# Two of a norm's four small steps move from GpSimd to VectorE

## The chip, the cores and the metric

The kernel runs on one core of one Trainium2 chip. The metric is the device time of one execution in microseconds. Engines are named as in the profile: PE is TensorE (PEld its weight loads), DVE is VectorE, ACT is ScalarE, POOL is GpSimd and SP is SyncE, which issues most DMAs.

## What is computed

The input x has 4 images of 128 channels and 64 x 64 places, so 4 x 4096 tokens of 128 channels. Two layers follow each other:

- Layer 0: a group norm, then `_L0_conv_ref`: a LayerNorm over channels, a depthwise 3x3 convolution with LayerNorm, GELU and a 1x1 product, a residual and a LayerNorm, then a state-space scan (16 states, 64 inner channels, four chunks of 32 channels) over the 4096 tokens, a LayerNorm, a projection, and a residual.
- Layer 1: LayerNorm, attention with 4 heads of 32 over the 4096 tokens of an image, a residual, LayerNorm, a mixture of 8 experts of which the best two count, and a residual.

What matters here is the LayerNorm without weights, which all of these use:

```python
def _layernorm(x, axis=-1, eps=1e-5):
    m = jnp.mean(x, axis=axis, keepdims=True)
    v = jnp.var(x, axis=axis, keepdims=True)
    return (x - m) / jnp.sqrt(v + eps)
```

## The kernel before

**Tiles.** The tokens of an image are cut into 8 blocks of 512. A block is held as 128 channels x 512 tokens, or, for norms, as 4 tiles of 128 tokens x 128 channels; TensorE transposes between the two. There are 32 blocks (4 images of 8).

**The norm.** `normalised(lane, src)` (line 502) handles one block. DVE makes statistics of the four tiles (`bn_stats` into st, then `bn_aggr` into mv, which holds a mean and a variance for each of the 4 tiles, so 128x4x2 numbers). POOL then makes the factor rs = (variance + EPS)^-0.5 and shift = -mean * rs, each 128x4 numbers, in four instructions: the addition of EPS to the variances (line 512, writes rs), the power with the constant tile mhalf (line 513, in place in rs), the product of mean and rs (line 515, writes shift) and the product of that with -1 (line 516, in place). The function then yields twice and ACT applies the norm to the four tiles with `scalar.activation(..., bias=shift, scale=rs)` (line 521) into xt, which TensorE transposes back. rs, shift, mv and st come from the pool `small` with 4 buffers of each name, and the names carry the lane's letter, X or Y.

Six places call it: `first_norm` (585), `conv` twice (638, 655), `closed` twice (804, 818) and `finished` (1032). Each is called for each of the 32 blocks, which makes 192 norms, 100 of them in lane Y and 92 in lane X.

**The scan's slot.** The work of the scan comes in 1024 units (block, half p, state n). One unit is one slot of the main loop (line 1223): ACT makes the decay da = exp(delta * A) (`decayed`, 742), DVE the product h = rows * du, the running scan over it and the product hc (`scan`, 747), TensorE sums hc over the 16 states in PSUM (y). From slot 128 on (`ALONE`, 1220) POOL first adds the hc of two states, and TensorE sums the pairs. ACT copies the last column of h into `state` for the next block.

**Attention** runs alongside: in each slot a group of two key tiles, with four score matmuls (sc), two exponentials on ACT (pT) and eight matmuls with values into av. It starts when blocks of an image are closed, so early in the kernel there is little of it.

**What sets the order.** Every call through `tensor`, `vector`, `scalar`, `gpsimd` and `sync` goes through `Queue` and `queued` (line 428), which chain the instructions of an engine in the order in which Python issues them. All records of these instructions bear line 445, so the text goes by tile names. The side work (norms, convolution, inputs of the scan, attention's inputs and outputs) is written as generators in two lanes, X and Y. `advance` (line 1137) runs a lane's generator to its next `yield`; each lane is advanced twice in a slot. The statistics and the four POOL instructions of a norm stand in one such stage, and ACT's four activations in the stage two yields later, which is one slot later.

So in DVE's queue the statistics of a norm stand between the scan work of two slots, and in POOL's queue the four small instructions stand between that engine's large ones: the pair sums of hc, the sums of avs, five operations of 128x512 for each input of the scan (du, ln, delta), zs, xr and tr.

Of the kernel before, what the change touches and what calls it, by code (L numbers as in the profile page):

```python
# [9 lines left out]
F32 = mybir.dt.float32  # L10
# [7 lines left out]
P = 128  # L18
C = 128
EPS = 1e-5  # L20
BLK = 512
NT = BLK // P
# [14 lines left out]
def conv_mamba_attn_moe_kernel(ctx: ExitStack, tc: tile.TileContext, t: dict):  # L37
# [8 lines left out]
    small = ctx.enter_context(tc.tile_pool(name="small", bufs=4))  # L46
# [127 lines left out]
    def any_scores(whole, tok):  # L174
# [111 lines left out]
        def layer1_any(o, t_tok, xa):  # L286
            with ExitStack() as es:
# [26 lines left out]
                with (  # L314
# [62 lines left out]
                    def closed(qb, sums):  # L377
# [18 lines left out]
                        tt = t_tok[:, NT * qb : NT * (qb + 1), :]  # L396
                        nc.vector.tensor_add(tt, ps, tt)
                        nc.scalar.copy(xf[:, qb * BLK : (qb + 1) * BLK], normalised(tt, psum))
                        ps = psum.tile([P, NT, NE], F32, tag="work", name="ps_r")
                        for j in range(NT):  # L400
# [38 lines left out]
    class Queue:  # L439
# [7 lines left out]
    tensor, vector, scalar, gpsimd, sync = (  # L447
        Queue(e) for e in (nc.tensor, nc.vector, nc.scalar, nc.gpsimd, nc.sync)
    )
# [40 lines left out]
    def tmp(lane, name, shape=None):  # L490
        return side.tile(shape or [P, BLK], F32, tag=f"tmp{lane}", name=name, bufs=4)
# [10 lines left out]
    def normalised(lane, src):  # L502


        st = small.tile([P, NT, 6], F32, name=f"st{lane}")
        mv = small.tile([P, NT, 2], F32, name=f"mv{lane}")
        for j in range(NT):
            vector.bn_stats(out=st[:, j, :], in_=src[:, j, :])
        for j in range(NT):
            vector.bn_aggr(out=mv[:, j, :], in_=st[:, j, :])  # L510
        rs = small.tile([P, NT], F32, name=f"rs{lane}")
        gpsimd.tensor_scalar_add(rs, mv[:, :, 1], EPS)
        gpsimd.tensor_tensor(rs, rs, mhalf, ALU.pow)
        shift = small.tile([P, NT], F32, name=f"shift{lane}")
        gpsimd.tensor_mul(shift, mv[:, :, 0], rs)
        gpsimd.tensor_scalar_mul(shift, shift, -1.0)
        yield
        yield
        xt = tmp(lane, "xt", [P, NT, C])
        for j in range(NT):  # L520
            scalar.activation(
                xt[:, j, :], src[:, j, :], AF.Identity, bias=shift[:, j : j + 1],
                scale=rs[:, j : j + 1],
            )
        yield
        return xt
# [47 lines left out]
    def first_norm(b, i, lane):  # L574
# [8 lines left out]
        ps = transposed(lane, by_tile(gn))  # L583
        yield
        xt = yield from normalised(lane, by_tile(ps))
        ps = transposed(lane, xt).rearrange(IMAGE, w=IMG)
        yield
# [21 lines left out]
    def conv(b, i):  # L609
# [26 lines left out]
        ps = transposed("Y", by_tile(cm))  # L636
        yield
        xt = yield from normalised("Y", by_tile(ps))
        ps = transposed("Y", xt)
        yield  # L640
# [743 lines left out]
```

## Time and profile before

| | before |
|---|---|
| median of 3 runs | 5564.33 us (5563.74 to 5565.13) |
| the profiled execution's own time | 5562.85 us |
| its span, first to last instruction | 5561.1 us |
| mean granted TensorE clock | 0.951 |
| bytes moved by DMA | 1131.52 MB, 203 GB/s |
| DVE instructions that aggregate a norm's statistics | 400 in lane Y, 368 in lane X, 153 ns each |
| ACT instructions that apply a norm | 400 in lane Y, 368 in lane X |

The profile is one execution. A row of a group gives the engine, the operation, the tiles written and read (out<-in), their shapes, how often it ran, then the busy time in us and the mean ns of one, and last the idle time of the engine just before it with what ended that idle time. A row of the waits gives who waited for whom, the sum in us, how often, and the longest. In the timeline the columns are the start in us, the length in us, the engine, the operation, and in square brackets the idle time before it. The chain of work that ended last is followed back from the last instruction, at each step to what released it or to the instruction before it on its engine.

Work is not the same all along. Until about 1000 us little attention is ready; PE is busy for 165 of the first 300 us and 571 of the next 700. From 1000 to 4000 us it is busy for 909 to 913 us of each 1000, DVE for 825 to 835, ACT for 751 to 771 and POOL for 446 to 464. After about 4800 us the scan is over and attention and the experts end.

### The profile page before, as it was taken

Reading aid. Unit: us, or ns where it says so; the run is one execution under the profiler, and the core shown is the slowest. Engines: PE = TensorE matmul, PEld = TensorE weight load, DVE = VectorE, ACT = ScalarE, POOL = GpSimd, SP = SyncE. Lnnn points to the kernel's source line nnn. Section 1 sums busy time; section 2 is a strip of 40 time slices with the busy share of each in tenths; the row PEclk is TensorE's granted clock in tenths of the full one; section 3 lists DMA queues with packets and bytes.
Section 4 is the critical chain, followed back from the end, with each engine's and each line's share of the span. In section 5 each row is a group of like instructions: output and inputs, shape, how many; then the busy total and the mean of one; then the engine's idle time right before and its main releaser. Section 6 shows DMA issues by size and latency. Waiting matters only on the chain.

```text
span 5561.1 us, 61179 instructions
## 1 busy us (share of the span) xinstructions
PE 4907.1 (88%) x17866; PEld 2045.2 (37%) x17866; DVE 4182.2 (75%) x6275; ACT 3897.4 (70%) x5989; POOL 2208.9 (40%) x1917
## 2 busy tenths in 40 slices
PE   4667798999899899999999999999899899999997
PEld 2223333333333333333333333333333333344443
DVE  4888778888887888888888888887888788862221
ACT  3455677788777777777877777777777777765553
POOL 2333445445434445444544444444544444421100
PEclk7778899999999999999999999999999999999998
DMA  2456566666665667667765667667765666754542
GB/s 92 169 172 193 185 205 230 215 222 229 228 206 192 228 201 255 216 204 243 249 208 193 209 214 242 219 210 234 249 207 196 207 221 203 249 193 168 168 146 67
DMA packets 451704, 1131.52 MB, mean 203 GB/s; under 512 B 51985, under 2 KB 135330, under 8 KB 451362
## 3 DMA queue, kind: packets, MB, share of 16 engines
q1 hardware_dynamic: 450194, 1126.74, 60.6%
q8 instruction: 144, 2.36, 0.2%
q14 instruction: 198, 1.62, 0.1%
q10 hardware_dynamic: 1168, 0.80, 0.0%
HBM read 967.12 MB, written 143.39 MB: 200 GB/s over the span
## 4 chain that ended last, share of the span: by engine, by line
PE 46%; DVE 18%; ACT 13%; DMA 7%; POOL 7%; issue 7%; SPq 1%; DVEq 0%; ACTq 0%; POOLq 0%
PE av L445 17%; PE sc L445 10%; DVE h L445 9%; PE ps_X L445 8%; PE ps_Y L445 6%; PE y L445 5%; ACT pT L445 4%; ACT xt L445 3%; ACT L445 2%; DMA rows<-bcd 2%; POOL rsY L445 2%; DMA ks<-kd 2%; DVE hc L445 2%; POOL rsX L445 1%; DVE cm L445 1%
## 5 line engine op out<-in xcount | busy, mean ns | idle before, releaser
L445 ACT ACTIVATE pT<-sc 128x1024 f32<-128x1024 f32 x2048 | 1982.2, 1021 | 965.6 <-PE sc L445 963.8
L445 PE MATMUL av<-pT,v 128*64 128x512 f32 x8192 | 2006.7, 611 | 3.7 <-ACT avs L445 3.5
L445 DVE TENSOR_TENSOR_SCAN h<-da,state,h 128x512 f32<-128x512 f32 x896 | 1339.2, 1495 | 106.7 <-ACT da L445 12.5
L445 PE MATMUL sc<-qs,ks 128*128 128x512 f32 x4096 | 1310.8, 440 | 110.9 <-ACT pT L445 55.0
L445 POOL TENSOR_TENSOR hc<-hc 128x512 f32<-128x512 f32 x448 | 641.6, 1434 | 1829.3 <-DVE hc L445 1669.9
L445 PEld LDWEIGHTS sc<-qs,ks 128*128 128x128 f32 x4096 | 716.7, 193 | 795.0 <-ACT pT L445 267.0
L445 PEld LDWEIGHTS av<-pT,v 128*64 128x64 f32 x8192 | 501.6, 137 | 1201.7 <-issue 1121.8
L445 DVE TENSOR_TENSOR h<-rows,du 128x512 f32<-128x512 f32 x1024 | 828.6, 809 | 65.0 <-POOL du L445 29.3
L445 DVE TENSOR_TENSOR hc<-rows,h 128x512 f32<-128x512 f32 x1024 | 807.7, 789 | 79.4 <-DVE h L445 2.3
L445 ACT ACTIVATE da<-delta,amat 128x512 f32<-128x512 f32 x1024 | 749.3, 732 | 15.8 <-DVE h L445 11.7
L445 PE MATMUL y<-hc,ident 128*128 128x512 f32 x1152 | 655.3, 656 | 68.3 <-DVE hc L445 37.7
L445 ACT ACT_TABLE_LOAD x319 | 409.3, 1283 | 18.1 <-PE ps_Y L445 13.0
L445 ACT COPY state<-h 128x1 f32<-128x1 f32 x896 | 175.3, 196 | 178.7 <-DVE h L445 178.3
L445 PEld LDWEIGHTS y<-hc,ident 128*128 128x128 f32 x1152 | 217.2, 206 | 208.9 <-DVE hc L445 74.1
L445 POOL TENSOR_TENSOR avs<-avs,prev 128x512 f32<-128x512 f32 x96 | 145.8, 1518 | 341.8 <-ACT avs L445 258.7
L445 POOL TENSOR_SCALAR rsY<-mvY 128x4 f32<-128x4 f32 x100 | 60.8, 608 | 490.4 <-DVE mvY L445 486.0
L445 DVE TENSOR_TENSOR share<-share,xf 128x1024 f32<-128x1024 f32 x128 | 180.6, 1411 | 92.2 <-DMA share<-sharesX 58.5
L445 PE MATMUL ps_X<-share,w_ew 128*128 128x512 f32 x432 | 215.9, 622 | 24.6 <-DVE share L445 24.5
L445 ACT ACTIVATE xt<-ps_Y,shiftY,rsY 128x128 f32<-128x128 f32 x380 | 143.0, 462 | 124.9 <-POOL shiftY L445 117.4
L445 ACT COPY avs<-av 128x512 f32<-128x512 f32 x160 | 94.1, 588 | 162.4 <-PE av L445 133.8
L445 POOL TENSOR_SCALAR du<-e 128x512 f32<-128x512 f32 x64 | 151.2, 2362 | 140.9 <-ACT e L445 140.8
L445 DVE TENSOR_TENSOR_SCAN h<-da,h 128x512 f32<-128x512 f32 x128 | 182.9, 1429 | 15.4 <-ACT da L445 2.6
(234 smaller groups left out, 4642.2 us busy)
## 6 DMA issues: line engine op xcount, KB each, us to landing
rows<-bcd SPq DMA_DIRECT2D x1024, 512.0 KB
ks<-kd SPq DMA_DIRECT2D x192, 512.0 KB
qs<-qd SPq DMA_DIRECT2D x161, 512.0 KB
share<-sharesX SPq DMA_DIRECT2D x108, 512.0 KB
v<-vd SPq DMA_DIRECT2D x192, 256.0 KB
ks<-kd SPq DMA_DIRECT2D x128, 256.0 KB
avd<-avs SPq DMA_DIRECT2D x96, 256.0 KB
prev<-avd SPq DMA_DIRECT2D x96, 256.0 KB
```

The lines of the kernel that those rows point to most:

```text
L445: return lambda *args, **kw: queued(op(*args, **kw))
```

## The change

The addition of EPS goes from POOL to DVE, right behind the aggregation. The sign is taken from the mean ahead of the product instead of from the product, in a DVE instruction of its own. POOL keeps the power and one product.

```diff
@@ -509,11 +509,11 @@
         for j in range(NT):
             vector.bn_aggr(out=mv[:, j, :], in_=st[:, j, :])
         rs = small.tile([P, NT], F32, name=f"rs{lane}")
-        gpsimd.tensor_scalar_add(rs, mv[:, :, 1], EPS)
+        vector.tensor_scalar_add(rs, mv[:, :, 1], EPS)
+        shift = small.tile([P, NT], F32, name=f"shift{lane}")
+        vector.tensor_scalar_mul(shift, mv[:, :, 0], -1.0)
         gpsimd.tensor_tensor(rs, rs, mhalf, ALU.pow)
-        shift = small.tile([P, NT], F32, name=f"shift{lane}")
-        gpsimd.tensor_mul(shift, mv[:, :, 0], rs)
-        gpsimd.tensor_scalar_mul(shift, shift, -1.0)
+        gpsimd.tensor_mul(shift, shift, rs)
         yield
         yield
         xt = tmp(lane, "xt", [P, NT, C])
```

In the order of the built programs, each of the 192 norms has two instructions more on DVE and two fewer on POOL; PE, ACT and SP have the same instructions in the same order. The name `normalised` occurs twice in the file: the one in `any_scores` (line 177) belongs to a branch that runs only when the scores could grow too large, and is not changed.

## The prediction

> **What bounds the kernel now.** I read the page first (engines, then the chain that ended last), then the groups of the GpSimd (POOL), then the waits by stage, then single norms in the timeline.
>
> ```profile
> PE 4907.1 (88%) x17866; PEld 2045.2 (37%) x17866; DVE 4182.2 (75%) x6275; ACT 3897.4 (70%) x5989; POOL 2208.9 (40%) x1917
> ...
> PE 46%; DVE 18%; ACT 13%; DMA 7%; POOL 7%; issue 7%; SPq 1%; DVEq 0%; ACTq 0%; POOLq 0%
> ```
>
> TensorE is the fullest engine, yet it holds under half of the chain: the rest is handing over between in-order queues. POOL is only 40% busy, but 7% of the chain (about 390 us) lies on it: its latency matters, not its throughput. The four small instructions of a norm are these (pow, add, mul, negate; Y lane 100 norms, X lane 92):
>
> ```profile
> L445 POOL TENSOR_TENSOR rsY<-rsY,mhalf 128x4 f32<-128x4 f32 x100 | 172.9, 1729 | 8.3
> ...
> L445 POOL TENSOR_SCALAR rsY<-mvY 128x4 f32<-128x4 f32 x100 | 60.8, 608 | 490.4 <-DVE mvY L445 486.0
> ...
> L445 POOL TENSOR_SCALAR shiftX<-shiftX 128x4 f32<-128x4 f32 x92 | 51.3, 558 | 8.1
> L445 POOL TENSOR_SCALAR rsX<-mvX 128x4 f32<-128x4 f32 x92 | 45.2, 492 | 190.9 <-DVE mvX L445 178.0 <-DVE prY L445 9.8
> ...
> L445 POOL TENSOR_SCALAR shiftY<-shiftY 128x4 f32<-128x4 f32 x100 | 30.6, 306 | 8.8
> ```
>
> Four numbers in a partition take 0.3 to 0.6 us in an add and 1.7 us in a power. Who pays for it is ScalarE (ACT), which applies the norm. Its waits in the first 1000 us, then from 1000 to 5000 us:
>
> ```profile
> ACT xt L445 <- POOL shiftY L445: 81.7, 19, 25.0
> ...
> ACT xt L445 <- POOL shiftX L445: 38.4, 7, 8.1
> ```
>
> ```profile
> ACT pT L445 <- PE sc L445: 703.9, 466, 8.8
> ...
> ACT xt L445 <- POOL shiftY L445: 35.7, 39, 2.2
> ```
>
> So 26 waits of 4.6 us on average early, where little attention is there to fill the gap, and 39 of 0.9 us later; in the other norms ACT arrives after POOL is done. The timeline of a norm whose wait is long:
>
> ```profile
> 414.92 0.36 DVE L445 BATCH_NORM_AGGREGATE mvY<-stY 128x2 f32<-128x6 f32 x4
> ...
> 415.20 0.66 DVE L445 TENSOR_TENSOR h<-rows,du 128x512 f32<-128x512 f32 x1
> ...
> 415.37 0.57 POOL L445 TENSOR_SCALAR rsY<-mvY 128x4 f32<-128x4 f32 x1 [6.35 <-DVE mvY L445]
> 415.96 1.28 DVE L445 TENSOR_TENSOR_SCAN h<-da,state,h 128x512 f32<-128x512 f32 x1
> 416.03 2.05 POOL L445 TENSOR_TENSOR rsY<-rsY,mhalf 128x4 f32<-128x4 f32 x1
> ...
> 418.16 0.48 POOL L445 TENSOR_TENSOR shiftY<-mvY,rsY 128x4 f32<-128x4 f32 x1
> ...
> 418.72 0.24 POOL L445 TENSOR_SCALAR shiftY<-shiftY 128x4 f32<-128x4 f32 x1
> ...
> 419.00 1.50 ACT L445 ACTIVATE xt<-ps_Y,shiftY,rsY 128x128 f32<-128x128 f32 x4 [4.67 <-POOL shiftY L445]
> ```
>
> From the last aggregation's end (415.28) to ACT is 3.72 us. The add ends when VectorE's (DVE's) product h ends; the power, issued into the scan, ends 0.84 us after the scan. POOL's steps are mostly waiting for the next gap between DVE's instructions. Compare a norm whose power was issued inside the product h:
>
> ```profile
> 963.13 0.69 DVE L445 TENSOR_TENSOR h<-rows,du 128x512 f32<-128x512 f32 x1 [0.19 <-issue]
> 963.34 1.38 POOL L445 TENSOR_TENSOR rsY<-rsY,mhalf 128x4 f32<-128x4 f32 x1
> 963.93 1.28 DVE L445 TENSOR_TENSOR_SCAN h<-da,state,h 128x512 f32<-128x512 f32 x1
> ...
> 964.79 0.41 POOL L445 TENSOR_TENSOR shiftY<-mvY,rsY 128x4 f32<-128x4 f32 x1
> ```
>
> Here the power gets in between product and scan, ends 0.90 us after the product, doesn't lengthen the scan (1.28 us in both), and the multiply ends with the scan.
>
> [...] the add takes 0.23 us with DVE quiet and 0.57 under the product, the power 1.04 and 2.05. [...] the trace has the like in gn, a DVE tensor_scalar of 0.54 us in the median and 1.56 at most. [...] The trace puts a one-column DVE tensor_scalar (gr) at 0.14 us; that is the price used.
>
> **The change, part by part.**
>
> *Removed from POOL*: add and negate, 60.8 + 45.2 + 30.6 + 51.3 = 188 us of 2209 busy. As POOL isn't full, this is worth only the latency that it takes from the norm. The power and one multiply stay.
>
> *Added to DVE*: 2 x 192 instructions, 384 x 0.14 = 54 us busy. In the queue: before, h starts 0.08 us ahead of the last aggregation's end (415.20 against 415.28). The epsilon add needs that result, so it can start 0.03 after the end (dependent small instructions at 35.42, 35.59 and 35.77 us follow each other at 0.17 to 0.18). The negation, independent, follows at the spacing of 34.12 to 34.22, about 0.08, and h another 0.08 on. h moves from -0.08 to about +0.18: 0.25 us a norm, 48 us in all. Bounds: 0.15 (two spacings, the wait hidden) to 1.2 [...] (gn's 1.56 less 0.54, and the pair). I take 0.25[...]. Behind the waiting add stand negation, h, scan and hc; for hc wait the y matmuls and POOL's pair sum, for h ACT's state copy.
>
> *Waits.* The built program's order shows that the epsilon add waits for DVE itself alone in 191 of 192 cases, so the reuse of rs and shift buffers costs nothing. POOL's power now waits for DVE's add, its multiply for DVE and for the power; the negation is done long before. No DMA and no TensorE instruction moves, and SyncE's and ACT's orders are unchanged.
>
> *Latency of a norm, DVE busy*: add ends at +0.17; POOL is released 0.09 later (the crossing seen at 415.28 to 415.37), at +0.26, when h (0.18 to 0.84) is running. That is the case of 963: the power ends at 0.84 + 0.90 = 1.74, the multiply is held to the scan's end (0.92 + 1.28 = 2.20), ACT starts at about 2.23. Before: 3.72. Saved: about 1.45 us. *DVE quiet* (four norms before 75 us): the add becomes 0.14 us faster, a multiply of 0.24 and its gap go: 0.45 us. So bounds for one norm are 0.45 and 1.5 us; more where two norms stand behind each other on POOL.
>
> *What of it counts.* Early: 26 waits, of which 4 x 0.45 = 2 us and 22 x 1.45 = 32 us. POOL's rs and shift lie on the chain there again and again, but so does DVE (12.5% for h), which is late next; I let 0.7 of the 32 through: 22 us. With the 2, 24 us. Later: a wait can't give more than it is. 36 us from 1000 to 5000 (plus some 6 on shiftX); ACT's next work is pT, which waits 704 us for TensorE's scores in this stage, so part of any ACT time is absorbed by that. I take half: 18 us. Cost: norms without a wait, about 192 - 66 = 126, delay DVE's stream by 0.25 us; DVE is on the chain for 18% of the span, so 126 x 0.25 x 0.18 = 6 us.
>
> Sum: 24 + 18 - 6 = 36 us less. The profiled execution took 5562.85 us (span 5561.1 and 1.75 around it), so about 5527; the median of the runs is 1.5 us above it, so 5528.
>
> **Rivals.**
>
> *All of it passes (0.15).* The chain runs over POOL's norms without a near second. Then early 34, later 42, nothing for DVE: 76 less, 5488. For it: POOL holds about 390 us of the chain, and TensorE's own time is 4907. Against: ACT is late anyway in most norms.
>
> *Hidden (0.13).* Early a third passes (11), later nothing, DVE costs 6: 5 less, 5559. For it: after 1000 us TensorE is over 90% busy and a 0.9 us wait sits beside its queue of matmuls.
>
> *Slower: DVE's stream sets the slots (0.14).* In each slot h, scan and hc come from DVE in order, and y, the pair sum and the state copy wait for them. If the stream is what ends a slot after 1000 us, the 156 norms there cost 156 x 0.25 = 39 us with no gain, and early only half of the expected 24 is kept: 39 - 12 = 27 more, 5591. It decides from the point where the early 12 are eaten: 12 of 39, so once about a third of the later pairs lie on the path while the later waits give nothing back. For it: DVE is 83% busy from 1000 to 4000 us. Against: POOL's hc waits 1574 us for DVE there without TensorE suffering much, so the stream has slack to TensorE.
>
> That the change doesn't do what it says can be left out: the built program has 384 more DVE and 384 fewer POOL instructions.
>
> **How the numbers follow.** Forecast (0.58): 5528, its own range 5508 to 5550 (pass shares of 0.5 to 1 early, 0.2 to 0.8 later). The range over all cases, 5486 to 5566, takes in the hidden case and the full one and leaves the slower one out. A change under 0.2%, 11 us, can't be told from none here. Faster by more: 0.58 + 0.15 + a little of the hidden case = 0.75; within: 0.11; slower: 0.14.
>
> **What would show it.** Right: POOL's power moves from mostly 2.0 to mostly 1.3 to 1.5 us; rs to xt about 2.2 us in the busy pattern; ACT's wait for shift falls from 161 us to well under 110, early waits from 4.7 to about 3.2; h starts 0.2 to 0.3 us after the last aggregation. Wrong: the DVE pairs at 0.5 us or more [...]; the power still at 2.0, having missed the gap ahead of the scan; or ACT's lost wait coming back as pT's wait for scores.

## The result, and the profile after

| | before | after |
|---|---|---|
| median | 5564.03 us (4 runs, 5555.20 to 5565.13) | 5489.67 us (4 runs, 5483.86 to 5494.46) |
| profiled execution | 5562.85 us, span 5561.1 | 5487.06 us, span 5485.3 |

The ratio is 0.987 (95% interval 0.9856 to 0.9885): 74 us less, about twice the 36 that were forecast. In the later batches the runs of before had medians of 5561 to 5565 us; each experiment is compared with those of its own batch.

The page of after, engines and chain:

```profile
PE 4887.0 (89%) x17866; PEld 2042.1 (37%) x17866; DVE 4325.5 (79%) x6659; ACT 3896.1 (71%) x5989; POOL 1950.6 (36%) x1533
...
PE 46%; DVE 24%; ACT 13%; issue 8%; DMA 7%; POOL 1%; SPq 1%; DVEq 0%; ACTq 0%; POOLq 0%
```

POOL went from 7% of the chain to 1%, DVE from 18% to 24%. POOL is 258 us less busy, DVE 143 us more, and PE 20 us less, though its matmuls are the same. Of DVE's 143 us the new pair accounts for about 70; the rest lies in instructions that were not touched, which take longer on average: hc 0.83 us against 0.79, gn 1.35 against 0.72, the scan 1.52 against 1.50. The norm's power in the groups of POOL:

```profile
L445 POOL TENSOR_TENSOR rsY<-rsY,mhalf 128x4 f32<-128x4 f32 x100 | 140.8, 1408 | 504.6 <-DVE shiftY L445 503.2
...
L445 POOL TENSOR_TENSOR rsX<-rsX,mhalf 128x4 f32<-128x4 f32 x92 | 112.4, 1222 | 232.8 <-DVE shiftX L445 232.0
```

It fell from 1.73 and 1.58 us to 1.41 and 1.22 without being touched. The timeline of the norm that the prediction showed at 415 us, now at 403:

```profile
402.50 0.36 DVE L445 BATCH_NORM_AGGREGATE mvY<-stY 128x2 f32<-128x6 f32 x4
...
402.89 0.17 DVE L445 TENSOR_SCALAR rsY<-mvY 128x4 f32<-128x4 f32 x1
...
402.97 0.16 DVE L445 TENSOR_SCALAR shiftY<-mvY 128x4 f32<-128x4 f32 x1
403.04 0.68 DVE L445 TENSOR_TENSOR h<-rows,du 128x512 f32<-128x512 f32 x1
...
403.14 1.45 POOL L445 TENSOR_TENSOR rsY<-rsY,mhalf 128x4 f32<-128x4 f32 x1 [6.55 <-DVE shiftY L445]
403.83 1.28 DVE L445 TENSOR_TENSOR_SCAN h<-da,state,h 128x512 f32<-128x512 f32 x1
...
404.67 0.44 POOL L445 TENSOR_TENSOR shiftY<-shiftY,rsY 128x4 f32<-128x4 f32 x1
...
405.14 1.51 ACT L445 ACTIVATE xt<-ps_Y,shiftY,rsY 128x128 f32<-128x128 f32 x4 [3.24 <-POOL shiftY L445]
```

From the aggregation's end (402.86) h starts at +0.18, the power at +0.28, it ends at +1.73, and ACT starts at +2.28 instead of +3.72. That is the working of the prediction to 0.05 us. So the effect on a norm of this kind was right, and the question is why the change was worth more.

**Where the time went.** The scan's slots mark the same work in both traces. The scan of slot 224 starts at 1034.1 us before and at 1006.4 after, the last one at 4969.2 and 4891.8 (so the scan runs on past the 4800 us named above), and the rest takes 591.9 and 593.5 us. So 28 us were won in the first stage (forecast: 24), 50 us in the second (forecast: 12) and nothing in the last. Busy times between the two marks, before and after (length of the stretch, then PE, PEld, DVE, ACT and POOL busy with their counts, granted clock, DMA):

```profile
1034.10:4969.20 3935.10, 3593.41 (x13428) 1494.94 (x13426) 3260.35 (x4730) 2980.72 (x4572) 1771.39 (x1491) 0.98 0.66 220
```

```profile
1006.40:4891.80 3885.40, 3574.96 (x13428) 1493.66 (x13426) 3376.48 (x5016) 2977.03 (x4570) 1578.25 (x1204) 0.98 0.67 222
```

PE's idle time fell from 342 to 310 us and its busy time by 18; together that is the 50. What PE waited for in the same stretch, before:

```profile
PE ps_Y L445 <- ACT xt L445: 42.1, 40, 2.5
...
PE ps_X L445 <- ACT xt L445: 30.4, 46, 5.4
...
PE y L445 <- POOL hc L445: 24.9, 23, 2.6
```

and after:

```profile
PE ps_X L445 <- ACT xt L445: 31.3, 41, 5.4
...
PE ps_X L445 <- DVE lo L445: 19.0, 23, 3.6
...
PE y L445 <- POOL hc L445: 1.6, 5, 0.6
```

PE's wait for ACT's xt in lane Y has left the list (1.5 us in all), and its wait for the pair sum hc is down to 1.6 us. Others grew: that for lo from 4.3 to 19.0 us, that for aT by 6 and that for prX by 4. So PE's idle time fell by 31 us only. In ACT's list the 35.7 us of waiting for shiftY (39 times) are gone too, while its wait for scores, which the prediction expected to swallow half of them, is 684.5 us before and 669.4 after. So three explanations were open: ACT's waits for the norm; the pair sums that stand behind the norm's small instructions on POOL; or that DVE's pair merely shifted the queues against each other.

### The profile page after: what moved, and what is told of

Its sections match the earlier page's. It is cut to its first block, busy times and chain, and to the rows that moved or that the text cites. A ratio compares the mean times of both kernels' runs of the same rounds, so it can differ in the third digit from the quotient of the medians.

```text
span 5485.3 us, 61265 instructions
## 1 busy us (share of the span) xinstructions
PE 4887.0 (89%) x17866; PEld 2042.1 (37%) x17866; DVE 4325.5 (79%) x6659; ACT 3896.1 (71%) x5989; POOL 1950.6 (36%) x1533
## 4 chain that ended last, share of the span: by engine, by line
PE 46%; DVE 24%; ACT 13%; issue 8%; DMA 7%; POOL 1%; SPq 1%; DVEq 0%; ACTq 0%; POOLq 0%
PE av L445 17%; DVE h L445 12%; PE sc L445 11%; PE ps_X L445 8%; PE ps_Y L445 5%; ACT pT L445 5%; PE y L445 4%; ACT xt L445 3%; DVE hc L445 2%; ACT L445 2%; DMA ks<-kd 2%; DMA rows<-bcd 2%; DMA inv<-inverse 1%; DVE cm L445 1%; ACT da L445 1%
## 5 line engine op out<-in xcount | busy, mean ns | idle before, releaser
L445 DVE TENSOR_TENSOR_SCAN h<-da,state,h 128x512 f32<-128x512 f32 x896 | 1358.5, 1516 | 106.0 <-ACT da L445 13.5
L445 POOL TENSOR_TENSOR hc<-hc 128x512 f32<-128x512 f32 x448 | 658.9, 1471 | 2024.6 <-DVE hc L445 1806.7
L445 DVE TENSOR_TENSOR hc<-rows,h 128x512 f32<-128x512 f32 x1024 | 852.2, 832 | 78.3 <-DVE h L445 2.3
L445 PE MATMUL y<-hc,ident 128*128 128x512 f32 x1152 | 644.0, 645 | 48.8 <-DVE hc L445 43.0
L445 POOL TENSOR_TENSOR rsY<-rsY,mhalf 128x4 f32<-128x4 f32 x100 | 140.8, 1408 | 504.6 <-DVE shiftY L445 503.2
L445 POOL TENSOR_TENSOR rsX<-rsX,mhalf 128x4 f32<-128x4 f32 x92 | 112.4, 1222 | 232.8 <-DVE shiftX L445 232.0
```

Of the source, the lines that this page charges most:

```text
L445: return lambda *args, **kw: queued(op(*args, **kw))
```

## The experiments

"Late" below is the stretch from the scan of slot 224 to the last scan, found in each trace.

**1. Half of the change: only the addition moves.**

```diff
-        gpsimd.tensor_scalar_add(rs, mv[:, :, 1], EPS)
+        vector.tensor_scalar_add(rs, mv[:, :, 1], EPS)
```

> Half of the change: the EPS addition is on VectorE, product and negation stay on GpSimd. Theory A (what counts is the time from the last aggregation to ScalarE, which goes in steps set by the gaps between VectorE's two-input instructions): the power is now issued inside the product h and ends about 0.9 us after it, at about 1.7 us; the multiply ends with the scan at about 2.15, the negation follows at 2.5 or, if caught by hc, at 2.9. So 0.8 to 1.2 of the 1.45 us are kept: 40 to 62 us faster than before. Theory B (what counts is how many small instructions GpSimd has to do): half of the 74 us, about 37, the same as for the other half. Power mostly 1.4 us under A.

Measured: 5484.46 us against 5564.90, ratio 0.9854 (0.9839 to 0.9869), 80 us faster. The power's median in lane Y is 1.42 us, as theory A says, but the gain is that of the whole change, which neither theory had. The gaps of theory A are in the trace of before: lane Y's power took 1.04 us in the median where it started with DVE idle (6 norms), 1.33 under the product h (24) and 2.05 under the scan (48); lane X's took 1.04 us under the statistics that DVE reads from ps_Y (20).

**2. The other half: only the sign moves.** The edit is against before; the allocation of shift, which moves up with it, is not shown.

```diff
+        vector.tensor_scalar_mul(shift, mv[:, :, 0], -1.0)
         gpsimd.tensor_tensor(rs, rs, mhalf, ALU.pow)
-        gpsimd.tensor_mul(shift, mv[:, :, 0], rs)
-        gpsimd.tensor_scalar_mul(shift, shift, -1.0)
+        gpsimd.tensor_mul(shift, shift, rs)
```

> The other half: the mean is negated on VectorE, GpSimd keeps the EPS addition, the power and one product. Theory A: the addition still waits for the product h and the power still falls into the scan and takes 2.05 us; only the last 0.33 us of 3.7 go, and h is about 0.08 us later. 5 to 25 us faster. Theory B: half of the 74 us, about 37.

Measured: 5484.83 us, ratio 0.9860 (0.9844 to 0.9875), again 80 us. Theory A had 5 to 25 and theory B 37: both miss. The timeline of the same norm tells why:

```profile
401.12 0.36 DVE L445 BATCH_NORM_AGGREGATE mvY<-stY 128x2 f32<-128x6 f32 x4
...
401.52 0.17 DVE L445 TENSOR_SCALAR shiftY<-mvY 128x4 f32<-128x4 f32 x1
...
401.57 0.23 POOL L445 TENSOR_SCALAR rsY<-mvY 128x4 f32<-128x4 f32 x1 [6.35 <-DVE mvY L445]
401.60 0.71 DVE L445 TENSOR_TENSOR h<-rows,du 128x512 f32<-128x512 f32 x1
...
401.88 1.31 POOL L445 TENSOR_TENSOR rsY<-rsY,mhalf 128x4 f32<-128x4 f32 x1
402.41 1.28 DVE L445 TENSOR_TENSOR_SCAN h<-da,state,h 128x512 f32<-128x512 f32 x1
...
403.72 1.50 ACT L445 ACTIVATE xt<-ps_Y,shiftY,rsY 128x128 f32<-128x128 f32 x4 [3.19 <-POOL shiftY L445]
```

One small DVE instruction ahead of h holds h back from -0.08 to +0.12 us, and POOL's addition, issued at +0.09, gets in ahead of it: 0.23 us instead of 0.57. The power then stands in the product and gets into the gap ahead of the scan. From the aggregation's end to ACT it is 2.24 us instead of 3.72; about 0.3 of that is the negation that is gone, so being 0.03 us earlier than h is worth about 1.1 us of latency. The mechanism of A holds; I had applied it wrongly to this kernel, by moving h by 0.08 us, less than the 0.09 that the crossing to POOL took at 415 us.

**3. DVE's pair alone.**

```diff
+        idle = small.tile([P, 2, NT], F32, name=f"idle{lane}")
+        vector.tensor_scalar_add(idle[:, 0, :], mv[:, :, 1], EPS)
+        vector.tensor_scalar_mul(idle[:, 1, :], mv[:, :, 0], -1.0)
```

> Before, and VectorE's two added instructions beside it, writing a tile that nobody reads: GpSimd still does all four. This is the price of the pair alone. The prediction's price: h 0.25 us later in 192 norms, of which 18% lie on the chain: 6 to 12 us slower. The prediction's rival (VectorE's stream sets the slots): 30 us or more slower. If it is under 6 us, the pair was free, and the missing part of the gain is smaller by that.

Measured: 5545.62 us, ratio 0.9964 (0.9950 to 0.9977): 19 us faster, with 384 instructions more and none fewer. By delaying h the pair does in part what experiment 2 did (lane Y's power has a median of 1.45 us against 1.99, but the addition still one of 0.52 against 0.57). Late, ACT still waits 38.5 us for POOL, and the late stage is only 8.5 us shorter. The prediction's slower rival falls. What the pair costs by itself can't be read here, since the run holds its price and the earlier norm together; the forecast 6 us could lie under the gain.

**4. After, with POOL's load put back behind the product.**

```diff
         gpsimd.tensor_mul(shift, shift, rs)
+        idle = small.tile([P, 2, NT], F32, name=f"idle{lane}")
+        gpsimd.tensor_scalar_add(idle[:, 0, :], rs, EPS)
+        gpsimd.tensor_scalar_mul(idle[:, 1, :], shift, -1.0)
```

> After, and two small GpSimd instructions of the same kind behind the product, writing a tile that nobody reads: GpSimd has as much to do as before, but the norm itself is as quick as after. Theory A for ScalarE's waits: 60 to 74 us faster than before. Rival (GpSimd's large instructions, the pair sums above all, stand behind the small ones, and that was the gain): only 10 to 40 us faster, and TensorE's y waits for the pair sum again, some 25 us from 1000 to 5000 us.

Measured: 5486.35 us, ratio 0.9858 (0.9843 to 0.9873), 79 us faster. What PE waited for late:

```profile
PE ps_X L445 <- ACT xt L445: 27.1, 41, 5.4
...
PE y L445 <- POOL hc L445: 16.1, 20, 1.8
```

PE waits 16 us for pair sums again (25 before, 1.6 after), POOL is 2141 us busy (2209 and 1951), and the time doesn't mind. POOL's load and its pair sums are ruled out.

**5 and 6. The change in one stage alone.** The edit chooses between the new lines and the old by the slot at which the norm is issued; experiment 6 has `slot >= 224` in the same place. Only the condition is shown.

```diff
+        if slot < 224:
```

> The change in the norms up to slot 224 of the scan alone (about the first 1000 us), the old four instructions later. By the start of the same scan in both traces the change won 28 us up to there. If stages add up: 25 to 31 us faster, close to the 24 of the prediction. If the early gain also makes the later stage better (another alignment of the queues), more than 40.

> The change in the norms from slot 224 on alone. By the same marks 48 us were won there. If stages add up: 43 to 51 us faster, four times the 12 that the prediction had for this stage (18 for half of the waits, less 6 for VectorE). If the late gain hangs on the earlier start or on another alignment: under 25.

Measured: early alone 5545.00 us against 5561.15, ratio 0.9971 (0.9960 to 0.9983), 16 us; late alone 5514.40, ratio 0.9922 (0.9908 to 0.9935), 43 us from the ratio and 47 from the medians. In the early kernel's trace 24 us are won by slot 224, as forecast, and 10 of them are lost again by slot 640. The late gain is there without the early one, so it doesn't hang on an earlier start. The two add up to 59 to 63 us, 11 to 15 less than the 74 of both together. With intervals of about 6 us on either side of the early gain and 8 on either side of the other two, that is hardly more than the scatter; the runs don't tell more.

**7. No power at all.** Against after, this kernel leaves out the power: rs is the constant 0.5.

```diff
-        vector.tensor_scalar_add(rs, mv[:, :, 1], EPS)
+        vector.tensor_scalar(rs, mv[:, :, 1], 0.0, 0.5, ALU.mult, ALU.add)
...
-        vector.tensor_scalar_mul(shift, mv[:, :, 0], -1.0)
-        gpsimd.tensor_tensor(rs, rs, mhalf, ALU.pow)
-        gpsimd.tensor_mul(shift, shift, rs)
+        vector.scalar_tensor_tensor(shift, mv[:, :, 0], -1.0, rs, ALU.mult, ALU.mult)
```

> Leaves out the power: rs is the constant 0.5, and VectorE makes rs and the product -mean x rs, so GpSimd has nothing to do in a norm. It tells what the rest of GpSimd's steps (2.28 us from the aggregation to ScalarE) still costs. Theory A: early norms lose about another 1.8 us each, 22 of them, so 25 to 40 us more; later the waits for GpSimd are already down to some 6 us, and with the pair sums at most 15 more. In all 100 to 125 us faster than before. Theory B (GpSimd's load): another 253 us of small work goes, after 258 us of less busy time gave 74, so some 145 us faster.

Measured: 5493.72 us, ratio 0.9868 (0.9850 to 0.9886): 67 to 73 us faster than before and no better than after, though a norm is mostly ready within 0.5 us. Both expectations miss. Late it had been clear that nothing was left (ACT's waits were 5.7 us). Early PE idles 15 us less than after (228 against 243 us up to slot 224), but is 18 us longer busy at a granted clock of 0.860 against 0.866. This kernel computes on other numbers; whether they bear on its clock was not tried.

**8 and 9. The norm made late again.** After, with two or four more powers ahead of the norm's own; DVE and the product as after. The edit with two is shown; the other has 4 in both places.

```diff
+        idle = small.tile([P, 2, NT], F32, name=f"idle{lane}")
+        for j in range(2):
+            gpsimd.tensor_tensor(idle[:, j, :], rs, mhalf, ALU.pow)
         gpsimd.tensor_tensor(rs, rs, mhalf, ALU.pow)
```

> After, with two more powers of GpSimd ahead of the norm's own, into a tile that nobody reads: the norm comes to about 4.2 to 4.6 us, as late as before, while VectorE's pair and the product stay as after. If ScalarE's late waits for GpSimd are the cause and pass in full: the waits from slot 224 to the last slot come back to about 40 us, TensorE's waits for xt there from 33 to over 70, and the time to within 10 us of before less what the pair won alone, 5540 to 5575 us. If the gain was another alignment of the queues through VectorE's pair: under 5515 us.

> The same with four powers ahead, so the norm comes at about 7 us, past the 4.5 to 5.7 us at which ScalarE gets to it. If the waits pass in full: nearly every late norm waits, 1 to 3 us each, 150 to 350 us in all, and the time rises by as much over after: 5640 to 5850 us. If TensorE's queue of scores takes up part of a wait, as the prediction had it: half of the added waits or less comes back as time.

Measured: 5669.96 us, ratio 1.0185 (1.0169 to 1.0200), and 6091.13 us, ratio 1.0960 (1.0942 to 1.0977). Both lie above what full passing gave. With two powers the norm is ready later than I had reckoned (5.5 us on average, not 4.2 to 4.6: 5.0 in lane X and 6.0 in lane Y, where a lane X norm's powers can stand ahead). With four, ACT waits late:

```profile
ACT xt L445 <- POOL shiftY L445: 235.2, 72, 5.3
ACT xt L445 <- POOL shiftX L445: 145.8, 72, 5.4
```

and PE, in the same stretch:

```profile
PE ps_Y L445 <- ACT xt L445: 184.3, 54, 4.7
...
PE ps_X L445 <- ACT xt L445: 181.6, 71, 9.2
```

The wait of ACT arrives at PE almost whole, 381 and 366 us. PE's whole idle time grows by less: against after, late, ACT waits 81 us longer with two powers and PE idles 82 us longer; with four it is 375 and 292. PE's wait for pair sums, 1.6 us after, is 34 us with two powers but only 17 with four, about as in experiment 4, so it isn't what makes the slowest kernel slow. The rest of the longer late stretch is busy time of PE, 49 and 138 us; the first stage is longer too, by 51 and 140 us. Neither was in the expectations.

**All kernels in the late stretch.** "Norm ready" is the mean time from the last aggregation's end to the end of POOL's last instruction of that norm (DVE's last in the kernel without the power); the waits are of ACT's xt for POOL and of PE for ACT's xt, in us; busy and length are PE's busy time and the length of the stretch.

| kernel | median us | norm ready | ACT waits | PE waits | PE busy | length |
|---|---|---|---|---|---|---|
| before | 5564 | 4.6 | 41 | 73 | 3593 | 3935 |
| DVE's pair alone | 5546 | 3.8 | 39 | 73 | 3589 | 3927 |
| addition alone | 5484 | 3.2 | 6 | 33 | 3575 | 3877 |
| sign alone | 5485 | 2.7 | 4 | 33 | 3572 | 3878 |
| POOL's load back | 5486 | 2.6 | 4 | 31 | 3578 | 3889 |
| after | 5490 | 2.1 | 6 | 33 | 3575 | 3885 |
| early alone | 5545 | 4.7 | 45 | 77 | 3597 | 3943 |
| late alone | 5514 | 2.1 | 7 | 33 | 3576 | 3886 |
| no power | 5494 | 0.6 | 0 | 31 | 3593 | 3895 |
| two powers first | 5670 | 5.5 | 87 | 113 | 3624 | 4016 |
| four powers first | 6091 | 8.3 | 381 | 366 | 3713 | 4315 |

The length goes with ACT's wait, not with POOL's load nor with the number of DVE instructions. The kernel without the power, on other numbers, is 10 us off through PE's busy time.

Which norms waited late is not what the norm at 415 us suggests. Of the 36 us in lane Y before, 31 lie on 39 norms that stand on POOL directly behind a norm of lane X. One of them, before (rows between left out):

```profile
3305.37 0.36 DVE L445 BATCH_NORM_AGGREGATE mvY<-stY 128x2 f32<-128x6 f32 x4
...
3306.49 1.24 POOL L445 TENSOR_SCALAR shiftX<-shiftX 128x4 f32<-128x4 f32 x1
...
3307.80 0.70 POOL L445 TENSOR_SCALAR rsY<-mvY 128x4 f32<-128x4 f32 x1
...
3310.77 1.50 ACT L445 ACTIVATE xt<-ps_Y,shiftY,rsY 128x128 f32<-128x128 f32 x4 [0.39 <-POOL shiftY L445]
```

Its statistics end at 3305.73, but POOL is still on the X norm, whose negation runs to 3307.73, and starts 2.07 us later. On average these 39 norms start on POOL 3.1 us after their statistics and are ready at 6.4 us before; they are ready at 5.6 us with DVE's pair alone, at 4.0 with the addition alone, at 3.7 with the sign alone and at 2.3 after, and ACT's waits for them are 31, 31, 2, 0 and 0 us. ACT comes to such a norm only some 4.3 to 5.4 us after its statistics, because xt is issued a slot later, so 4.0 us is early enough and a quicker norm brings nothing. That is why either half was as good as the whole. None of these versions beats after by more than the runs scatter.

## Why the prediction was wrong in size

- **What bounds the kernel, and the local mechanism: right.** POOL's latency counted, through the gaps between DVE's instructions. Forecast for a busy norm: h at +0.18, power's end at +1.74, ACT at +2.23; measured +0.18, +1.73, +2.28. One pair of lines was misread on the way: 34.12 to 34.22 is a spacing of 0.10 us, not 0.08; in the norm at 403 us it was 0.08 and 0.07.
- **Early stage: right in the sum, with some luck.** 24 us forecast, 24 and 28 by the slot marks. ACT's early waits fell by 44 us (120 to 76) where 34 were expected, and a smaller share of that passed: 24 to 28 of 44, not 0.7. One of these waits, 25 us long, is the first norm's and hardly changed; the others were 3.8 us on average before, not 4.6, and 2.5 after.
- **Late stage: this step failed.** It said: "ACT's next work is pT, which waits 704 us for TensorE's scores in this stage, so part of any ACT time is absorbed by that. I take half: 18 us." Almost nothing was absorbed. PE's instructions are issued in a fixed order, and the transposes of xt stand ahead of later matmuls, so while ACT waits for POOL, the fullest engine of the stage waits for ACT. The list of PE's waits had it, with 106 us for xt in lane Y over the whole run; I went by the spare time of the engine that waits, where the question was who waits for it. Measured: PE's late wait for xt fell from 73 to 33 us with ACT's from 41 to 6, and PE's idle time fell by 31 us where ACT's wait fell by 35. The prediction named two norms behind each other on POOL as a case beside its bounds; late it was the main one, and as it took a wait to give no more than it is, that didn't change its sum.
- **And a term was missing.** Between the marks PE's busy time falls by 18 us as well. Before minus after is then 18 of busy and 31 of idle time, 50 in all, where the waits alone were worth 41 at most. With the waits put back the busy time rises again, to 3624 and 3713 us.
- **DVE's cost, 6 us: not seen.** That POOL wouldn't make a norm's 0.25 us longer was an estimate, with 1.2 us as its bound. The pair itself behaves about as priced (medians of 0.17 and 0.16 us against 0.14, h 0.26 us later), and few of the pairs took longer: 12 of 192 EPS additions over 0.3 us, the longest 1.21, and no negation over 0.18. Experiment 3 is faster than before, so a net cost is ruled out there, a small one under the gain is not. (Waits came 72 times, 58 in lane Y and 14 in lane X, so the sum should have had 120 norms, not 126: 5.4 us.) But the prediction's 54 us of added busy time became 143: the pair moved POOL's instructions against DVE's large ones as well. gn, for one, starts under POOL's product ln in 24 of 32 cases (median 1.49 us), where before it started under the tensor_scalar du in 21 (median 0.54). After, h took 1.76 us in the median where it started under a POOL operation on two tiles of 128x512 other than the pair sum (117 times), and 0.68 with POOL idle (780). What this cost in time wasn't separated.
- **The rivals.** "All of it passes" gave 5488 us and hits the time, though its parts are other ones: 34 and 42 us forecast, 28 and 50 measured. That the total fits is luck, since it has no term for PE's busy time. The shares behind the forecast's own range give an upper end of about 5545, not 5550. "Hidden" is refuted by the late kernel, "DVE's stream sets the slots" by DVE's pair alone.
- **The signs.** Power down to 1.2 to 1.4 us: yes. ACT's wait for shift under 110: 107 us in all. Early waits 3.2 us on average: 76 us in 21, 3.6.

What stays open: whether the early gain and the late one bring more together than apart, what moves PE's busy time, why the early gain partly runs off in the early kernel, and why no gain came from taking out the power early.

## What to carry to other kernels

Before a wait on an engine with spare time is discounted, read the waits of the fullest engine, and who ends them: here ACT's late wait fell by 35 us and PE's idle time by 31. POOL's chain had a latency in steps here, a power of 1.04, 1.33 or 2.05 us by what DVE was running: ask into which gap of the neighbour each instruction of such a chain falls, since in experiment 2 h 0.20 us later was worth about 1.1 us of latency. Look for the case in which two such chains stand behind each other: here it made most of the late waits. And a latency paid here only until the consumer's own arrival, 4.3 to 5.4 us after the statistics: half of this change, either half, would have done.

## What was not expected of the hardware

PE's busy time for the same matmuls of the late stretch (13,426 to 13,430 are recorded) goes with its idle time: 3575 us where PE idles 310 us (mean granted clock 0.978 in that stretch), 3593 at 342 (0.975), 3624 at 393 (0.966), 3713 at 602 (0.930). Busy time times granted clock is 3496, 3505, 3499 and 3455 us, so the longer busy time comes for the most part with the lower clock. In these kernels a longer stall of PE thus came with a loss beyond its length: with four powers first, PE idles 292 us longer than after and is busy 138 us longer. Whether the idle time lowers the granted clock was not tried; the kernel without the power has 302 us of idle time and yet 3593 us of busy time at 0.972, on other numbers.

POOL's small instructions took longer under DVE's large ones: the addition at 415 us, under h, took 0.57 us, the one at 401 us in experiment 2, ahead of h, 0.23. The other way round, the power shows nothing of this: in the trace of after, 131 scans start while a power is running, and none takes more than 1.29 us, as with POOL idle (median 1.28). The 147 that start under a pair sum of 128x512 take 2.11 us in the median.
